# A selective scan that goes through two states in one instruction, over two adjacent PSUM banks

## The chip, the cores and the metric

The kernel runs on one core of a Trainium2 chip. The time is the device time of one execution in microseconds (us). A core has five engines with an instruction queue each, which run side by side and wait for one another through semaphores: TensorE (PE) multiplies matrices into PSUM, VectorE (DVE) and ScalarE (ACT) work on SBUF and PSUM, GpSimd (POOL) works on SBUF only, and SyncE (SP) here issues all DMAs. Each queue is worked off in order: an instruction that waits holds up everything behind it on its engine.

## What is computed

Eight images of 96 channels and 64x64 points go through a hybrid block: layer norm, projection, depthwise convolution, a selective scan in four directions, gating, two small convolutions with a channel gate, then a linear attention and a feed-forward layer in 8-bit floats. Most of the time goes into the scan, which for every direction k, channel d (192) and state n (16) runs over the 4096 points:

```python
def step(hst, inp):
    u_i, dt_i, b_i, c_i = inp
    dA = jnp.exp(dt_i[..., None] * A)
    hst = dA * hst + (dt_i * u_i)[..., None] * b_i[:, :, None, :]
    y = jnp.einsum('bkdn,bkn->bkd', hst, c_i)
    return (hst, y)
...
ys = ys.transpose(1, 2, 3, 0) + D[None, :, :, None] * u
```

with `dt_i` a softplus of a projection (the step sizes, `delta`), and `A = -exp(A_logs)`. The four directions are forward and backward over two orders of the points; their results are added.

## The kernel before

**Units.** The scan part works in 256 units in a row: 8 images x 4 directions x 8 chunks of T = 512 points. A chunk continues the states of the chunk before it in its direction, except the first of each direction (`u.start`, 32 units). Channels lie 64 to a tile, and the two halves of the 128 partitions hold two different states of them; so 192 channels x 16 states are 24 rows of [128, 512], worked off in 24 **slots**. Slot 4n + m is state m (of G = 4) of tile n (of 6, `TILES`).

**One state.** ACT makes the decays `da` = exp(delta x A) into a PSUM bank (`decays`, L1062), two slots ahead of their use, into one of three banks in turn. POOL makes the scan's inputs `hb` = b x du for the four states of a tile at once (`inputs`, L946, into one of six buffers). DVE scans (L1123): h = da x h + hb along the 512 points; a backward unit walks the row from its end. The product with C is made in one of two ways. A **banked** state is scanned into its PSUM bank and multiplied by c on DVE into `hb` (L1125); an unbanked one is scanned into `hb`, and POOL multiplies all unbanked states of a tile together (`outputs`, L952). `BANKED` says how many states of each tile are banked: tiles 0, 2 and 4 wholly, 1 and 3 not at all, tile 5 one or two, which makes 13 banked states in the first 8 units of all images but the first, and 14 in all others. The last column of each state is kept by ACT in `carry` (L1126 for one banked state, L1131 for the unbanked states of a tile), for the next chunk. PE sums `hb` over states and halves into the banks y01 and y2 (`sums`, L972), adds the skip term or the other directions' result (L981, fetched by `before`), and ACT copies them out (`gather`, L989 and L992).

**Step sizes.** `step_sizes` has six parts: PE's matmul into a bank of its own, `dt` (L911), three ACT activations (L919, L921, L923), one DVE operation that reads the bank again (L925), and one POOL product with u (L928). Form "a" serves a unit, form "b" the last 64 channels of two units. `spread` copies the results by DMA to both halves (L940).

**Order.** Nothing is scheduled automatically: each engine gets its instructions in the order of the program. `plan` puts every step of a unit at a slot by hand; in each slot the scan comes first, then the planned steps, then one step of each **side stream**: the front of the next image and the back end of the last one (convolutions, norms, attention, feed-forward) are generators that yield how many slots to pause. They use the banks f0 and f1. [...]da 3, dt 1, f0, f1, y01, y2.

**DMA.** SP issues fetches in the program's order, and requests made with `later` three slots after.

Of the kernel before, what the change touches and what calls it, by code (L numbers as in the profile page):

```python
# [22 lines left out]
T = 512  # L23
# [7 lines left out]
SPREAD = 5  # L31
HB = 6

BANKED = ((4, 0, 4, 0, 4, 1), (4, 0, 4, 0, 4, 2))

HOLD = 3
LAND = 11
# [6 lines left out]
def kernel(ctx: ExitStack, tc: tile.TileContext, a, out):  # L44
# [13 lines left out]
    dram = ctx.enter_context(tc.tile_pool(name="scratch", bufs=2, space=DRAM))  # L58
    psum = ctx.enter_context(tc.tile_pool(name="psum", bufs=1, space=PSUM))

    BANKS = {"da": 3, "dt": 1, "f0": 1, "f1": 1, "y01": 1, "y2": 1}

    def bank(tag, name):
        return psum.tile([P, T], F32, tag=tag, name=name, bufs=BANKS[tag])
# [9 lines left out]

    eps = const([P, 1], 1e-5, "eps")
    one = const([P, 1], 1.0, "one")
    ones_c = const([C, C], 1.0 / C, "ones_c")

    def centering(n, m, diagonal, name):
# [766 lines left out]
    for b in range(out.shape[0]):  # L846
        s = {"b": b, "done": set(), "live": b + 1 == out.shape[0]}
        images.append(s)
        for pair in (1, 0):
            for back in range(2):  # L850
                for i in range(NC):
                    u = Unit()
                    u.s, u.pair, u.back, u.k = s, pair, back, pair + 2 * back
                    u.c, u.start = (NC - 1 - i if back else i), i == 0
                    u.new, u.i = (pair, back, i) == (1, 0, 0), len(units)
                    u.bc, u.hb, u.delta, u.du = {}, {}, {}, {}
                    u.banked = BANKED[int(b == 0 or u.i % 32 >= NC)]
                    units.append(u)

# [41 lines left out]
    def step_sizes(us, i):  # L901

        u, which = us[0], "ab"[len(us) - 1]
        if i == 0:
            u.ps = bank("dt", "dt")
            if which == "a":
                todo = [(u.ps, slice(0, P), u)]
            else:
                todo = [(u.ps[64 * h : 64 * h + 64], slice(P, DI), w) for h, w in enumerate(us)]
            for ps, d, w in todo:  # L910
                nc.tensor.matmul(ps, dt_w[32 * w.k : 32 * w.k + R + 1, d], w.dts, start=True, stop=True)  # L911
            u.nat = sp.tile([P, T], F32, tag="nat" + which, name="nat", bufs=1)
            if which == "a":
                u.nata = u.nat
            else:
                for w in us:
                    w.natb = u.nat
        elif i == 1:
            nc.scalar.activation(u.nat, u.ps, AF.Abs)  # L919
        elif i == 2:  # L920
            nc.scalar.activation(u.nat, u.nat, AF.Exp, scale=-1.0)  # L921
        elif i == 3:
            nc.scalar.activation(u.nat, u.nat, AF.Ln, bias=one)  # L923
        elif i == 4:
            nc.vector.scalar_tensor_tensor(u.nat, u.ps, 0.0, u.nat, ALU.max, ALU.add)  # L925
        else:
            x = u.ua if which == "a" else u.ub
            nc.gpsimd.tensor_tensor(x, u.nat, x, ALU.mult)  # L928
# [19 lines left out]
    def outputs(u, n):  # L948

        lo = u.banked[n]  # L950
        hb = u.hb[n][:, lo:, :]
        nc.gpsimd.tensor_tensor(hb, hb, u.bc[1, TILES[n][0]][:, lo:, :], ALU.mult)  # L952

    def before(u):

        src = u.s["u"][1] if u.k == 1 else u.s["y"][u.pair]
        u.plain = []
        for i, rows in enumerate((slice(0, P), slice(P, src.shape[0]))):
            t = sp.tile([P, T], F32, tag=f"u{i}", name=f"u{i}", bufs=1)[: rows.stop - rows.start]
            u.plain.append(into(t, src[rows, bass.ts(u.c, T)]))  # L960

    def sums(u, ns, m):

# [7 lines left out]
        for ps, n, i in todo:  # L971
            nc.tensor.matmul(  # L972
                ps, halves, u.hb[n][:, i, :], start=TILES[n][0] == 0 and m == 0, stop=False, skip_group_check=True
            )
        if ns[-1] == 5 and m == 1:
            first = u.k == 1
            for ps, w, x in (
                (u.p[0], dd_a if first else ident, u.plain[0]),
                (u.p[1][low] if first else u.p[1], dd_b if first else ident, u.plain[1]),
            ):  # L980
                nc.tensor.matmul(ps, w, x, start=False, stop=True, skip_group_check=True)  # L981

    def gather(u, i):

# [12 lines left out]
    def plan(u, last, nxt, third):  # L997

        at = [[] for _ in range(24)]

        def put(slot, f, *args):
            at[slot].append((f, args))

        if last:
            put(0, outputs, last, 5)
            put(0, before, last)
            for m in range(2):
                put(m, sums, last, (3, 4), 2 + m)
            for m in range(2):
                put(5 + m, sums, last, (5,), m)  # L1010
            put(7, states, u, 1, 1)
            put(10, gather, last, 0)
            put(11, gather, last, 1)
        for n in range(6):
            to = (u, n + 2) if n < 4 else (nxt, n - 4)
            if to[0]:
                put(4 * n + 1, inputs, *to)
        if third and u.i % 2:
            put(16, step_sizes, (nxt, third), 5)
        put(8, outputs, u, 1)  # L1020
        put(16, outputs, u, 3)
        for m in range(4):
            put(13 + m, sums, u, (0, 1), m)
            if m < 2:
                put(18 + m, sums, u, (2,), m)
                put(22 + m, sums, u, (3, 4), m)
        if nxt:
            for i, slot in enumerate((0, 2, 4)):
                put(slot, step_sizes, (nxt,), i + 3)
            put(4, spread, nxt, 0, (0, 1))  # L1030
            put(6, spread, nxt, 1, (0, 1))
            put(10, states, nxt, 0, 0)
            put(15, states, nxt, 1, 0)
            put(20, states, nxt, 0, 1)
            if u.i % 2 == 0:
                put(15, spread, nxt, 0, (2,))
                put(16, spread, nxt, 1, (2,))
        if third:
            put(1, fetched_dt, third)
            put(9, fetched_u, third)  # L1040
            for i, slot in enumerate((20, 22, 23)):
                put(slot, step_sizes, (third,), i)
            if u.i % 2:
                for i, slot in enumerate((9, 11, 12, 13, 15)):
                    put(slot, step_sizes, (nxt, third), i)
                put(17, spread, nxt, 0, (2,))
                put(18, spread, nxt, 1, (2,))
            elif u.i + 3 < len(units):
                put(21, fetched_pair, third, units[u.i + 3])
        return at  # L1050

    def at_index(i):
        return units[i] if 0 <= i < len(units) else None

    def decays(q):

        if q >= 24 * len(units):
            return
        u, (n, m) = units[q // 24], divmod(q % 24, G)
        g, j = TILES[n]  # L1060
        da[q] = bank("da", "da")
        nc.scalar.activation(  # L1062
            da[q], u.delta[j], AF.Exp, scale=a_neg[:, u.k, j, g * G + m : g * G + m + 1]
        )

    da, kept, side, carry = {}, [], [], None
    for u in units[:2]:
        fetched_dt(u)
    fetched_u(units[0])
# [6 lines left out]
    for what in range(2):  # L1076
        spread(units[0], what, range(3))
    fetched_u(units[1])
    for i in range(3):
        step_sizes(units[1:2], i)  # L1080
    inputs(units[0], 0)
    inputs(units[0], 1)
    decays(0)
    decays(1)

    def advance(n):

# [4 lines left out]
    for u in units:  # L1092
        last, nxt, third = (at_index(u.i + d) for d in (-1, 1, 2))
        if u.new:
# [7 lines left out]
            else:  # L1102
                final = back_end(b, u.s)
                last_kit = back_kit(None, "f0", True, kit_f)
                side.append(Stream(final[0][0](last_kit, range(1, NC)[::-1])))
        if third and third.new:
            drained(*side[-1:])
            all_issued()
        if u.start:
            carry = sp.tile([P, 24], F32, tag="carry", name="carry")  # L1110
        todo = plan(u, last, nxt, third)
        for slot in range(24):
            n, m = divmod(slot, G)
            g, j = TILES[n]
            q, hb, first_at = 24 * u.i + slot, u.hb[n], 0 if u.back else T - 1
            col = carry[:, 8 * j + g * G + m : 8 * j + g * G + m + 1]
            while kept:
                kept.pop(0)()
            decays(q + 2)
            d = da.pop(q)  # L1120
            banked = m < u.banked[n]
            dd, x = (d[:, ::-1], hb[:, m, ::-1]) if u.back else (d, hb[:, m, :])
            nc.vector.tensor_tensor_scan(dd if banked else x, dd, x, 0.0 if u.start else col, ALU.mult, ALU.add)  # L1123
            if banked:
                nc.vector.tensor_tensor(hb[:, m, :], d, u.bc[1, g][:, m, :], ALU.mult)  # L1125
                kept.append(lambda col=col, d=d, at=first_at: nc.scalar.copy(col, d[:, at : at + 1]))  # L1126
            elif m == G - 1:
                lo = 8 * j + g * G
                kept.append(
                    lambda c=carry[:, lo + u.banked[n] : lo + G].unsqueeze(2), h=hb[:, u.banked[n] :, :], at=first_at:  # L1130
                    nc.scalar.copy(c, h[:, :, at : at + 1])  # L1131
                )
            for f, args in todo[slot]:
                f(*args)
            place[0] = slot
# [2 lines left out]
    for f in kept:  # L1138
        f()
    outputs(u, 5)  # L1140
    before(u)
    for m in range(2):
        sums(u, (3, 4), 2 + m)
    for m in range(2):
        sums(u, (5,), m)
    gather(u, 0)
    gather(u, 1)
    all_issued()
# [76 lines left out]
```

## Time and profile before

| | us |
|---|---|
| median of 3 runs (lowest to highest) | 11356.66 (11348.54 to 11358.43) |
| the profiled execution | 11372.37 |
| its span, first to last instruction | 11370.7 |
| the scan part in it | 347 to 11090 |
| one image of 32 units, in the middle | 1352 (2990 to 4342) |
| DMA, share of the 16 engines, scan part | 0.85 |
| PE clock granted, mean | 0.82 |

A profile line of a group names the source line, the engine, the operation, output <- inputs and their shapes and the count; after the first bar the total busy time in us and the mean duration in ns; after the second the idle time of the engine just before these instructions and what ended most of it. A line in order of time begins with the start and the duration in us; "x4" at its end are four in a row. A waiting line reads: who waited, at which line, <- for whom, then total us, number of times and the longest.

### The profile page before, as it was taken

The numbers are of one execution on the slowest core, as the hardware profiler recorded it, in microseconds if no ns is written. First come the engines' busy times: TensorE is split into PE (matmuls) and PEld (weight loads), VectorE is DVE, ScalarE is ACT, GpSimd is POOL, SyncE is SP. The second block draws the span as 40 slices with busy tenths as digits, with TensorE's granted clock in tenths as the row PEclk, the third lists the DMA queues.
The fourth block names the chain that finished last, engine by engine and source line by source line (L and its number), as shares of the span: only waits on it lengthen the run. The fifth ranks groups of instructions, "written<-read, shape, count | busy, mean of one in ns | idle before, by whom it ended". The sixth has DMA issues, their size and how long they took to land. (4 is left out here: it accounts for less than half of the span.)

```text
span 11370.7 us, 97041 instructions
## 1 busy us (share of the span) xinstructions
PE 8567.3 (75%) x23270; PEld 2328.5 (20%) x23270; DVE 10367.4 (91%) x10828; ACT 7508.4 (66%) x14939; POOL 10398.7 (91%) x2783
## 2 busy tenths in 40 slices
PE   6577657887778877888678876788768887676677
PEld 2111112222122211222112221222212221111122
DVE  0799999999999999999999999999999999999991
ACT  3566656767666676667766676666766667666674
POOL 0799999999999999999999999999999999999990
PEclk8678778888788877889778887888878888787787
DMA  2788878898888888888888888889888888888872
GB/s 71 171 197 197 201 189 210 209 225 196 203 210 212 219 198 202 210 215 215 195 207 210 216 214 194 210 205 228 202 200 211 212 220 195 198 198 195 201 188 78
DMA packets 1081039, 2253.24 MB, mean 198 GB/s; under 512 B 419609, under 2 KB 420314, under 8 KB 949395
## 3 DMA queue, kind: packets, MB, share of 16 engines
q1 hardware_dynamic: 1080467, 2247.05, 81.3%
q8 instruction: 184, 3.01, 0.1%
q14 instruction: 388, 3.18, 0.1%
HBM read 1507.14 MB, written 336.69 MB: 162 GB/s over the span
## 5 line engine op out<-in xcount | busy, mean ns | idle before, releaser
L946 POOL TENSOR_TENSOR hb<-b,du 128x2048 f32<-128x2048 f32 x1536 | 6939.0, 4535 | 21.3 <-DMA du<-ua 14.3
L1062 ACT ACTIVATE da<-delta,w_a_logs 128x512 f32<-128x512 f32 x6144 | 4216.7, 689 | 696.3 <-DVE hb L1123 575.8
L972 PE MATMUL p<-hb,halves 128*64 128x512 f32 x12288 | 3822.7, 731 | 800.1 <-POOL hb L952 382.1
L1123 DVE TENSOR_TENSOR_SCAN da<-da,carry,hb 128x512 f32<-128x512 f32 x3087 | 3949.0, 1279 | 58.0 <-ACT da L1062 54.3
L952 POOL TENSOR_TENSOR hb<-hb,c 128x2048 f32<-128x2048 f32 (+2 forms) x768 | 2984.9, 3887 | 304.7 <-ACT carry L1131 252.2
L1123 DVE TENSOR_TENSOR_SCAN hb<-da,carry,hb 128x512 f32<-128x512 f32 x2289 | 2781.0, 1264 | 57.7 <-ACT da L1062 56.7
L1125 DVE TENSOR_TENSOR hb<-da,c 128x512 f32<-128x512 f32 x3528 | 2440.5, 692 | 154.0 <-DVE da L1123 0.9
L1126 ACT COPY carry<-da 128x1 f32<-128x1 f32 x3528 | 554.9, 157 | 2351.6 <-DVE hb L1125 2341.1
L972 PEld LDWEIGHTS p<-hb,halves 128*64 128x64 f32 x12288 | 916.2, 161 | 3540.7 <-issue 2129.5
L434 PE MATMUL conv<-f0im,taps 97*128 97x512 f32 (+1 forms) x2088 | 903.5, 664 | 95.9 <-ACT f0pre L490 54.3
L928 POOL TENSOR_TENSOR ua<-nat,ua 128x512 f32<-128x512 f32 x256 | 327.3, 1279 | 257.5 <-DMA b<-xd 257.5
L1123 DVE TENSOR_TENSOR_SCAN da<-da,hb 128x512 f32<-128x512 f32 x441 | 537.7, 1219 | 26.0 <-POOL hb L946 24.6
L925 DVE SCALAR_TENSOR_TENSOR nat<-dt,nat 128x512 f32<-128x512 f32 x384 | 259.5, 676 | 238.9 <-ACT nat L923 238.9
L911 PE MATMUL dt<-dts,dt_w 7*64 7x512 f32 (+1 forms) x1024 | 450.0, 657 | 16.9 <-DVE nat L925 12.4
L981 PE MATMUL p<-u,ident 128*128 128x512 f32 x768 | 438.3, 699 | 3.6 <-DMA u<-y 3.6
L376 PE MATMUL ctr<-f1b,cen_c 96*96 96x512 f32 x460 | 271.9, 697 | 193.4 <-DVE f1b L769 158.8
L434 PEld LDWEIGHTS conv<-f0im,taps 97*128 97x128 f32 (+1 forms) x2088 | 254.6, 174 | 681.6 <-issue 523.5
L1123 DVE TENSOR_TENSOR_SCAN hb<-da,hb 128x512 f32<-128x512 f32 x327 | 377.9, 1204 | 4.9 <-ACT da L1062 4.9
L382 PE MATMUL var<-f1b,ones_c 96*96 96x512 f32 x346 | 207.4, 684 | 153.6 <-ACT f1b L379 145.3
L792 POOL TENSOR_TENSOR f1b<-f1b,f1o 96x512 f32<-96x512 f32 x58 | 67.7, 1167 | 252.0 <-ACT f1o L790 251.9
L1131 ACT COPY carry<-hb 128x4 f32<-128x4 f32 (+2 forms) x768 | 146.8, 191 | 197.4 <-DVE hb L1123 184.8
L655 PE MATMUL cab<-f1m,cab_w 96*96 96x512 f32 x348 | 206.0, 719 | 90.9 <-ACT f1b L664 41.4
(416 smaller groups left out, 7710.5 us busy)
## 6 DMA issues: line engine op xcount, KB each, us to landing
b<-xd SPq DMA_DIRECT2D x1024, 512.0 KB
c<-xd SPq DMA_DIRECT2D x1024, 512.0 KB
delta<-nat SPq DMA_DIRECT2D x1536, 128.0 KB
du<-ua SPq DMA_DIRECT2D x1024, 128.0 KB
y<-yt SPq DMA_DIRECT2D x512, 256.0 KB
u<-y SPq DMA_DIRECT2D x384, 256.0 KB
ua<-u SPq DMA_DIRECT2D x256, 256.0 KB
du<-ub SPq DMA_DIRECT2D x512, 128.0 KB
```

Of the source, the lines that this page charges most:

```text
L376: nc.tensor.matmul(ps, cen_c, src, start=i == 0, stop=i == len(srcs) - 1)
L434: nc.tensor.matmul(ps, taps[:, t, lo : lo + n], im[:, r0 + dy : r0 + dy + 8, dx : dx + HW], start=t == 0, stop=t == 8,)
L911: nc.tensor.matmul(ps, dt_w[32 * w.k : 32 * w.k + R + 1, d], w.dts, start=True, stop=True)
L928: nc.gpsimd.tensor_tensor(x, u.nat, x, ALU.mult)
L946: nc.gpsimd.tensor_tensor(hb, u.bc[0, g], u.du[j].unsqueeze(1).to_broadcast([P, G, T]), ALU.mult)
L952: nc.gpsimd.tensor_tensor(hb, hb, u.bc[1, TILES[n][0]][:, lo:, :], ALU.mult)
L972: nc.tensor.matmul(ps, halves, u.hb[n][:, i, :], start=TILES[n][0] == 0 and m == 0, stop=False, skip_group_check=True)
L981: nc.tensor.matmul(ps, w, x, start=False, stop=True, skip_group_check=True)
L1062: nc.scalar.activation(da[q], u.delta[j], AF.Exp, scale=a_neg[:, u.k, j, g * G + m : g * G + m + 1])
L1123: nc.vector.tensor_tensor_scan(dd if banked else x, dd, x, 0.0 if u.start else col, ALU.mult, ALU.add)
L1125: nc.vector.tensor_tensor(hb[:, m, :], d, u.bc[1, g][:, m, :], ALU.mult)
L1126: kept.append(lambda col=col, d=d, at=first_at: nc.scalar.copy(col, d[:, at : at + 1]))
```

## The change

Two neighbouring states (slots q and q + 1, q even) become one piece of work. The decays of a pair lie in one PSUM tile of two adjacent banks, and there are two such tiles, four banks; the bank `dt` is given up, and the step sizes' matmul uses y01 (form "a") or y2 (form "b") in the slots between the copy-out of the last unit's sums and the first sums of this one. One scan instruction runs over both states, 1024 elements. So that the second state in walking order doesn't continue the first, ACT sets the decay at its first point to zero, after it has put that point's share of the kept state into the input: hb += decay x carry (one-element Identity with pointers for scale and bias, then a one-element copy of a zero). In a starting unit there is no kept state and no Identity. A banked pair's product is one instruction over 1024 elements, and its two last columns are kept by one copy. `decays(q + 2)` still stands ahead of the scan of slot q, and so makes the next pair. `BANKED` goes to 14 banked states in the first 8 units of all images but the first and 16 elsewhere, where tile 5 is banked wholly and its `outputs` falls away. In `plan` the copies-out go from slots 10 and 11 to 5 and 8, the step sizes of form "a" into the slots 7 to 20 of one unit, and the fetches that feed them, the spreads and the fetch of the plain results (split in two) to other slots.

```diff
-BANKED = ((4, 0, 4, 0, 4, 1), (4, 0, 4, 0, 4, 2))
+BANKED = ((4, 0, 4, 0, 4, 2), (4, 0, 4, 0, 4, 4))
...
-    BANKS = {"da": 3, "dt": 1, "f0": 1, "f1": 1, "y01": 1, "y2": 1}
+    BANKS = {"f0": 1, "f1": 1, "y01": 1, "y2": 1}
...
-            u.ps = bank("dt", "dt")
+            u.ps = bank({"a": "y01", "b": "y2"}[which], "dt")
...
     def outputs(u, n):
         lo = u.banked[n]
+        if lo == G:
+            return
...
-        da[q] = bank("da", "da")
-        nc.scalar.activation(
-            da[q], u.delta[j], AF.Exp, scale=a_neg[:, u.k, j, g * G + m : g * G + m + 1]
-        )
+        d = da[q] = psum.tile([P, 2, T], F32, tag="da", name="da", bufs=2)
+        for i in range(2):
+            scale = a_neg[:, u.k, j, g * G + m + i : g * G + m + i + 1]
+            nc.scalar.activation(d[:, i, :], u.delta[j], AF.Exp, scale=scale)
+        i, at = (0, T - 1) if u.back else (1, 0)
+        edge, at = d[:, i, at : at + 1], slice(at, at + 1)
+        if not u.start:
+            x, col = u.hb[n][:, m + i, at], column(j, g, m + i)
+            nc.scalar.activation(x, edge, AF.Identity, bias=x, scale=carry[0][:, col : col + 1])
+        nc.scalar.copy(edge, zero)
...
+    def scanned_pair(u, slot):
+        n, m = divmod(slot, G)
+        g, j = TILES[n]
+        q, hb = 24 * u.i + slot, u.hb[n]
+        end = slice(0, 1) if u.back else slice(T - 1, T)
+        while kept:
+            kept.pop(0)()
+        decays(q + 2)
+        d, x = da.pop(q), hb[:, m : m + 2, :]
+        banked = m < u.banked[n]
+        dd, xx = (t.rearrange("p m l -> p (m l)") for t in (d, x))
+        if u.back:
+            dd, xx = dd[:, ::-1], xx[:, ::-1]
+        col = column(j, g, m + u.back)
+        init = 0.0 if u.start else carry[0][:, col : col + 1]
+        nc.vector.tensor_tensor_scan(dd if banked else xx, dd, xx, init, ALU.mult, ALU.add)
+        if banked:
+            nc.vector.tensor_tensor(x, d, u.bc[1, g][:, m : m + 2, :], ALU.mult)
+            states_of, lo, hi = d, m, m + 2
+        elif m == G - 2:
+            states_of, lo, hi = hb[:, u.banked[n] :, :], u.banked[n], G
+        else:
+            return
+        to = carry[0][:, column(j, g, lo) : column(j, g, hi)].unsqueeze(2)
+        kept.append(lambda: nc.scalar.copy(to, states_of[:, :, end]))
...
 # in plan: slots of the steps that move
-            put(0, before, last)
+            put(3, added, last, 0)
+            put(5, gather, last, 0)
...
+            put(6, added, last, 1)
+            put(8, gather, last, 1)
...
-            put(10, gather, last, 0)
-            put(11, gather, last, 1)
+            put(2, spread, nxt, 0, (0, 1))
+            put(3, spread, nxt, 1, (0, 1))
...
+            put(6, fetched_u, third)
+            for i, slot in enumerate((7, 9, 10, 11, 13, 20)):
+                put(slot, step_sizes, (third,), i)
+            if u.i % 2:
+                for i, slot in enumerate((9, 11, 12, 13, 15, 16)):
+                    put(slot, step_sizes, (nxt, third), i)
...
-        for m in range(4):
-            put(13 + m, sums, u, (0, 1), m)
+        for m, slot in enumerate((14, 15, 16, 16)):
+            put(slot, sums, u, (0, 1), m)
...
+        put(19, before, u, 0)
+        put(21, before, u, 1)
...
-            for i, slot in enumerate((0, 2, 4)):
-                put(slot, step_sizes, (nxt,), i + 3)
-            put(4, spread, nxt, 0, (0, 1))
-            put(6, spread, nxt, 1, (0, 1))
...
-            put(1, fetched_dt, third)
-            put(9, fetched_u, third)
-            for i, slot in enumerate((20, 22, 23)):
-                put(slot, step_sizes, (third,), i)
...
+            put(14, fetched_dt, fourth)
...
-            for f, args in todo[slot]:
+            if slot % 2 == 0:
+                scanned_pair(u, slot)
+            for f, args in todo[slot]:
```

`added` is the identity matmul of the plain results, which stood at the end of `sums` before.

More of the change, by code (lines that the diff above doesn't have):

```diff
@@ L76 @@
     one = const([P, 1], 1.0, "one")
+    zero = const([P, 1], 0.0, "zero")
     ones_c = const([C, C], 1.0 / C, "ones_c")
@@ L855 @@
                     u.new, u.i = (pair, back, i) == (1, 0, 0), len(units)
-                    u.bc, u.hb, u.delta, u.du = {}, {}, {}, {}
+                    u.bc, u.hb, u.delta, u.du, u.plain = {}, {}, {}, {}, {}
                     u.banked = BANKED[int(b == 0 or u.i % 32 >= NC)]
@@ L950, in outputs, with before, added @@
         lo = u.banked[n]
+        if lo == G:
+            return
         hb = u.hb[n][:, lo:, :]
         nc.gpsimd.tensor_tensor(hb, hb, u.bc[1, TILES[n][0]][:, lo:, :], ALU.mult)
-    def before(u):
+    def before(u, i):
         src = u.s["u"][1] if u.k == 1 else u.s["y"][u.pair]
[L957 to L960, printed above, removed]
+        rows = (slice(0, P), slice(P, src.shape[0]))[i]
+        t = sp.tile([P, T], F32, tag=f"u{i}", name=f"u{i}", bufs=1)[: rows.stop - rows.start]
+        u.plain[i] = into(t, src[rows, bass.ts(u.c, T)])
+    def added(u, i):
+        ps, first = u.p[i], u.k == 1
+        w = ((dd_a, dd_b)[i]) if first else ident
+        nc.tensor.matmul(
+            ps[0:64] if first and i else ps, w, u.plain[i], start=False, stop=True, skip_group_check=True
+        )
     def sums(u, ns, m):
@@ L974, in sums @@
             )
[L975 to L981, printed above, removed]
     def gather(u, i):
@@ L1005, in plan @@
             put(0, outputs, last, 5)
-            put(0, before, last)
             for m in range(2):
                 put(m, sums, last, (3, 4), 2 + m)
+            put(3, added, last, 0)
+            put(5, gather, last, 0)
             for m in range(2):
                 put(5 + m, sums, last, (5,), m)
+            put(6, added, last, 1)
+            put(8, gather, last, 1)
             put(7, states, u, 1, 1)
-            put(10, gather, last, 0)
-            put(11, gather, last, 1)
+        if nxt:
+            put(2, spread, nxt, 0, (0, 1))
+            put(3, spread, nxt, 1, (0, 1))
+        if third:
+            put(6, fetched_u, third)
[4 more added lines that the diff above has]
+                    put(slot, step_sizes, (nxt, third), i)
         for n in range(6):
@@ L1017, in plan @@
                 put(4 * n + 1, inputs, *to)
-        if third and u.i % 2:
-            put(16, step_sizes, (nxt, third), 5)
         put(8, outputs, u, 1)
         put(16, outputs, u, 3)
-        for m in range(4):
-            put(13 + m, sums, u, (0, 1), m)
+        for m, slot in enumerate((14, 15, 16, 16)):
+            put(slot, sums, u, (0, 1), m)
             if m < 2:
@@ L1037, in plan @@
                 put(16, spread, nxt, 1, (2,))
-        if third:
-            put(1, fetched_dt, third)
-            put(9, fetched_u, third)
-            for i, slot in enumerate((20, 22, 23)):
-                put(slot, step_sizes, (third,), i)
-            if u.i % 2:
-                for i, slot in enumerate((9, 11, 12, 13, 15)):
-                    put(slot, step_sizes, (nxt, third), i)
+            else:
                 put(17, spread, nxt, 0, (2,))
                 put(18, spread, nxt, 1, (2,))
-            elif u.i + 3 < len(units):
-                put(21, fetched_pair, third, units[u.i + 3])
+        fourth = at_index(u.i + 3)
+        if fourth:
+            put(14, fetched_dt, fourth)
+            if u.i % 2 == 0:
+                put(21, fetched_pair, third, fourth)
         return at
@@ L1053, in at_index, with column @@
         return units[i] if 0 <= i < len(units) else None
+    def column(j, g, m):
+        return 8 * j + g * G + m
     def decays(q):
@@ L1060, in decays @@
         g, j = TILES[n]
-        da[q] = bank("da", "da")
-        nc.scalar.activation(
-            da[q], u.delta[j], AF.Exp, scale=a_neg[:, u.k, j, g * G + m : g * G + m + 1]
-        )
-    da, kept, side, carry = {}, [], [], None
+        d = da[q] = psum.tile([P, 2, T], F32, tag="da", name="da", bufs=2)
[8 more added lines that the diff above has]
+        nc.scalar.copy(edge, zero)
+    da, kept, side, carry = {}, [], [], [None]
     for u in units[:2]:
@@ L1078 @@
     fetched_u(units[1])
-    for i in range(3):
-        step_sizes(units[1:2], i)
     inputs(units[0], 0)
@@ L1083 @@
     decays(0)
-    decays(1)
+    for i in range(6):
+        step_sizes(units[1:2], i)
+    fetched_dt(units[2])
+    def scanned_pair(u, slot):
[19 more added lines that the diff above has]
+            states_of, lo, hi = hb[:, u.banked[n] :, :], u.banked[n], G
+        else:
+            return
+        to = carry[0][:, column(j, g, lo) : column(j, g, hi)].unsqueeze(2)
+        kept.append(lambda: nc.scalar.copy(to, states_of[:, :, end]))
     def advance(n):
@@ L1105 @@
                 side.append(Stream(final[0][0](last_kit, range(1, NC)[::-1])))
-        if third and third.new:
+        if u.i + 3 < len(units) and units[u.i + 3].new:
             drained(*side[-1:])
@@ L1109 @@
         if u.start:
-            carry = sp.tile([P, 24], F32, tag="carry", name="carry")
+            carry[0] = sp.tile([P, 24], F32, tag="carry", name="carry")
         todo = plan(u, last, nxt, third)
         for slot in range(24):
[L1113 to L1132, printed above, removed]
+            if slot % 2 == 0:
+                scanned_pair(u, slot)
             for f, args in todo[slot]:
@@ L1140 @@
     outputs(u, 5)
-    before(u)
     for m in range(2):
@@ L1145 @@
         sums(u, (5,), m)
+    for i in range(2):
+        added(u, i)
     gather(u, 0)
```

## The prediction

> **What bounds the kernel now.** I read the page's first part, then busy times by stretch of one image, then groups by shape, then the order of time on VectorE (DVE), then the waits.
>
> ```profile
> PE 8567.3 (75%) x23270; PEld 2328.5 (20%) x23270; DVE 10367.4 (91%) x10828; ACT 7508.4 (66%) x14939; POOL 10398.7 (91%) x2783
> ```
>
> Two engines stand at 91%. The scan part runs from 347 to 11090 us, 10,743 us for 256 units, and the rest (627 us) is prelude and end, which the change leaves alone. One image (32 units) in quarters of 8 units:
>
> ```profile
> core 0: us, PE busy (x) PEld busy (x) DVE busy (x) ACT busy (x) POOL busy (x), PEclk, DMA share, GB/s
> 2990.00:3340.00 350.00, 272.52 (x676) 70.32 (x672) 329.77 (x344) 228.01 (x467) 332.21 (x86) 0.84 0.85 209
> 3340.00:3674.00 334.00, 281.21 (x838) 72.19 (x838) 318.73 (x328) 232.07 (x443) 321.76 (x85) 0.88 0.88 214
> 3674.00:4016.00 342.00, 280.97 (x806) 83.46 (x806) 324.98 (x346) 234.42 (x477) 320.66 (x86) 0.86 0.87 214
> 4016.00:4342.00 326.00, 228.44 (x592) 57.57 (x592) 320.64 (x331) 240.83 (x485) 325.72 (x92) 0.75 0.82 196
> ```
>
> After the stretch and its length the columns are busy time and, in brackets, instructions. DVE and POOL are both at 93.7% or more in every quarter; in the last one POOL is full (325.7 of 326) and DVE all but. ACT stands near 70%. Prices, from the groups by shape:
>
> ```profile
> L946 POOL TENSOR_TENSOR hb<-b,du 128x2048 f32<-128x2048 f32 x1536 | 6939.0, 4535 | 21.3 <-DMA du<-ua 14.3
> L1062 ACT ACTIVATE da<-delta,w_a_logs 128x512 f32<-128x512 f32 x6144 | 4216.7, 689 | 696.3 <-DVE hb L1123 575.8
> L1126 ACT COPY carry<-da 128x1 f32<-128x1 f32 x3528 | 554.9, 157 | 2351.6 <-DVE hb L1125 2341.1
> ```
>
> Durations overlap or leave gaps, so I take steps from start to start:
>
> ```profile
> 3411.29 1.28 DVE L1123 TENSOR_TENSOR_SCAN da<-da,carry,hb 128x512 f32<-128x512 f32 x1
> 3412.60 0.69 DVE L1125 TENSOR_TENSOR hb<-da,c 128x512 f32<-128x512 f32 x1
> 3413.21 1.28 DVE L1123 TENSOR_TENSOR_SCAN da<-da,carry,hb 128x512 f32<-128x512 f32 x1
> ...
> 3432.74 4.80 DVE L1123 TENSOR_TENSOR_SCAN hb<-da,carry,hb 128x512 f32<-128x512 f32 x4
> 3437.46 1.26 DVE L1123 TENSOR_TENSOR_SCAN da<-da,carry,hb 128x512 f32<-128x512 f32 x1
> ```
>
> A banked state (scan into PSUM, product with C on DVE) takes 1.31 + 0.61 = 1.92 us of DVE; an unbanked one (product on POOL) 4.72/4 = 1.18. A unit with 14 banked states takes 14 x 1.92 + 10 x 1.18 = 38.7 us, plus 1.5 step-size operations of 0.6, plus 1 to 2 us of the other streams: 40.5 to 41 against the 40.8 to 43.7 of the quarters. POOL, in the same order of time: eight operations at 4.48 (two inputs in a row took 8.97), one over two states at 2.33, 1.5 step-size products at 1.23: 40.0. What DVE and ACT wait for:
>
> ```profile
> DVE hb L1123 <- ACT da L1062: 61.6, 90, 1.4
> DVE da L1123 <- ACT da L1062: 54.3, 22, 6.0
> ...
> ACT carry L1126 <- DVE hb L1125: 2341.1, 2311, 4.1
> ```
>
> The columns are total us, times and longest. Today ACT waits for DVE; DVE waits for decays only 116 us.
>
> [...]
>
> **The change, part by part.**
>
> *Pairs on DVE.* A second state in the same instruction costs only its length. Banked pair: (1.31 + 1.07) + (0.61 + 0.53) = 3.52 instead of 3.84. Unbanked pair: 1.18 + 1.07 = 2.25 instead of 2.36. BANKED moves work from POOL too: 200 units go from 14 to 16 banked states, 56 units (3528 = 200 x 14 + 56 x 13) from 13 to 14. DVE per unit: 38.7 to 8 x 3.52 + 4 x 2.25 = 37.2 in the 200; 37.9 to 7 x 3.52 + 5 x 2.25 = 35.9 in the 56. Sum: 200 x 1.52 + 56 x 2.05 = 419 us less. All of it is on the path. No run shows a 1024 scan over two banks; if the fixed part were per element, 0 would be saved in pairing, and the moved products would cost (456 x 0.74) 340 us more.
>
> *POOL.* The 2.33 operation goes from 200 units and a 3.4 becomes 2.33 in 56: 528 us less, 37.7 and 40.0 per unit. It falls below DVE in the 200. In the 56, DVE has 35.9 + 0.9 + about 3 of the back end, so both stay level.
>
> *ACT, the added work.* Per pair one 1-element Identity with two pointers ([...]the 157 ns of the copy bounds it below; I take 0.35; none in the 32 starting units, so 2688) and one 1-element copy of zero (0.19, as the carry copies from SBUF), 3072. Carry copies fall from 3528 to 1992. Sum 941 + 584 - 292: about +1.2 ms on 7.3 ms, 80% of the scan part. Busy time alone costs nothing.
>
> *ACT, the added wait.* This is the disputed term. Before, three single banks: a decay had two slots to be made in. After, two double banks: those of pair p+1 start when pair p-1 is finished (product included), and are due when p ends. Chain: 0.62 + 0.70 (two decays, the second drained) + 0.35 + 0.19 + two handshakes of 0.04 = 1.94 us, 2.13 with the carry copy before it. DVE gives it 3.52 in a banked pair, 2.25 in an unbanked one. Behind it in ACT's queue stand all evacuations, norms and step-size activations (0.77 us per pair on average: 7284 - 4217 - 701 over 3072), and DVE stands behind it. A norm (two activations, 1.2 us) or Silu with two table loads (1.28 each, 1.48) does not fit beside an unbanked pair. Laying ACT's list beside DVE's in the changed order: ACT's is longer in 996 of 3060 pairs, by 858 us together; what even the slack of the following pair can't take up is 189. These are the ends. Arrears of neighbouring pairs add up and ACT also waits for PE (195 us today), so I take twice the lower, 380; the 116 of today are in it, so +265.
>
> *Identity waits for POOL's hb one pair earlier.* Behind it stand the zero copy and DVE. In the stretch after 3398 the tightest tile is ready 4.1 us ahead of its scan (3419.7 against 3423.9); the Identity comes 2.2 us ahead at most. Cost 0; if POOL is late by more, each microsecond is on the path (25 us today, most at the start).
>
> *Step sizes in y01/y2.* The matmul at slot 7 waits for the evacuation at slot 5, p's first matmuls at slot 14 for DVE's operation at slot 13. Behind the latter on PE are the sums that free hb for POOL at slot 17. POOL waits 7 us for them today. I take 0; its end is 2 us in each of 256 units. The dt fetch, u fetch and the plain-y fetches are only moved earlier or a slot pair away on SP, whose waits for nat (1952 us) go; nothing is due there. DMA stands at 0.85 share and would go to 0.86.
>
> *Side streams.* They advance in both slots of a pair, so half of their DVE operations directly follow ACT work of the same pair. DVE waits some 145 us for those now; I add a third, 45.
>
> Sum: -419 + 265 + 45 = -109. The profiled execution took 11372.4 us (span 11370.7), so 11263; it lies 16 above the median of 11356.7, so 11245.
>
> **Rivals.**
> 1. Forecast: DVE's saving arrives, two thirds are eaten by ACT. 11245 (11130 to 11330). Chance 0.45.
> 2. ACT keeps ahead, as its 66% suggest: -419 and hardly any new stall, 10960. Against it: 2.25 against 1.94. Chance 0.17.
> 3. ACT's chain becomes the bound in the unbanked tiles: the whole 858 is paid, less today's 116, plus 45: 11357 - 419 + 787 = 11725 at worst; 463 of the 858 lie in banked pairs, and with half of that absorbed it is 11494. I take 11500. It decides from 419 + 116 = 535 us of DVE waits for ACT, 2.1 per unit. For it: DVE waits up to 6 us for a decay already today. Chance 0.28, slower.
> 4. Pairing saves no DVE time, or PE's later sums bind POOL: the gain of 419 is void, about 11357. [...] Chance 0.10.
>
> **How the numbers follow.** A run can tell 0.2%, 23 us, from no change. Faster: 0.42 of rival 1, all of 2, 0.01 of 4: 0.60. Same: 0.03 + 0.02 + 0.05 = 0.10. Slower: 0.26 + 0.04 = 0.30. The range goes from the full saving (10950) to a little above rival 3, where a third of the banked pairs' 463 is absorbed (11571, cut to 11560).
>
> **What would show it.** Right: scans of 1024 at 2.35 us (products 1.22), 3072 of them; POOL at least 1 us per unit freer in the later quarters; DVE waiting 300 to 450 us for ACT, most in slots 4 to 7 and 12 to 15. Wrong: those waits under 200 or over 535 us; scans over 2.5 us; POOL or PE waits of more than 100 us more than now.

## The result, and the profile after

| | us |
|---|---|
| before, median of 4 runs (lowest to highest) | 11357.55 (11348.54 to 11363.57) |
| after, median of 4 runs (lowest to highest) | 11542.52 (11536.19 to 11544.22) |
| ratio, 95% interval | 1.0163 (1.0145 to 1.018) |
| profiled execution after, its span | 11542.72, 11541.0 |

The changed kernel is 1.6% slower; the forecast was 1.0% faster. The time lies within the range, but on the other side of no change.

The page's first line of the kernel after: PE, DVE and POOL have less to do, and ACT more.

```profile
PE 8504.1 (74%) x23270; PEld 2330.4 (20%) x23270; DVE 10069.0 (87%) x6221; ACT 8816.3 (76%) x18963; POOL 9883.1 (86%) x2583
```

DVE fell from 10367.4 to 10069.0 us and POOL from 10398.7 to 9883.1, yet the span grew. Over the scan part alone, now 347 to 11260 us:

```profile
core 0: us, PE busy (x) PEld busy (x) DVE busy (x) ACT busy (x) POOL busy (x), PEclk, DMA share, GB/s
347.00:11260.00 10913.00, 8086.50 (x22186) 2191.55 (x22186) 9987.35 (x6074) 8573.68 (x18594) 9841.86 (x2545) 0.82 0.82 202
```

The same view of before, over 347 to 11090:

```profile
347.00:11090.00 10743.00, 8143.79 (x22236) 2185.41 (x22238) 10311.60 (x10696) 7283.64 (x14612) 10376.00 (x2748) 0.82 0.85 205
```

So DVE is busy for 324 us less and idle for 495 us more (926 against 431): 171 us longer. The short gaps ahead of the products shrank by 54 us as well (from 154 to 100, the idle times at the end of these two lines, before and after):

```profile
L1125 DVE TENSOR_TENSOR hb<-da,c 128x512 f32<-128x512 f32 x3528 | 2440.5, 692 | 154.0 <-DVE da L1123 0.9
```

```profile
L1122 DVE TENSOR_TENSOR hb<-da,c 128x1024 f32<-128x1024 f32 x1992 | 2440.0, 1225 | 100.1 <-issue 0.4
```

So the real new waiting is 495 + 54 = 549 us. One image in quarters of 8 units, chosen at the same work as those of before:

```profile
3036.00:3388.00 352.00, 269.06 (x662) 71.81 (x662) 314.96 (x197) 266.93 (x593) 318.66 (x84) 0.82 0.82 206
3388.00:3734.00 346.00, 276.51 (x838) 72.02 (x838) 313.39 (x187) 275.15 (x571) 305.78 (x78) 0.90 0.85 207
3734.00:4079.00 345.00, 281.97 (x812) 84.35 (x814) 314.37 (x202) 274.02 (x599) 300.88 (x78) 0.86 0.83 210
4079.00:4415.00 336.00, 220.76 (x598) 56.60 (x594) 312.57 (x187) 283.93 (x607) 311.49 (x85) 0.78 0.78 193
```

No engine is full any more: DVE stands at 89 to 93% of a quarter where it had 94 to 98%, and POOL at 87 to 93%. The 27 us that this image loses lie in all its quarters, though unevenly (2, 12, 3 and 10 us), and are not one event. The groups of the pair's instructions, by shape:

```profile
L1120 DVE TENSOR_TENSOR_SCAN da<-da,carry,hb 128x1024 f32<-128x1024 f32 x1743 | 4096.1, 2350 | 272.7 <-ACT da L1082 118.0
...
L1120 DVE TENSOR_TENSOR_SCAN hb<-da,carry,hb 128x1024 f32<-128x1024 f32 x945 | 2206.7, 2342 | 319.6 <-ACT da L1082 302.8
...
L1129 ACT COPY carry<-da 128x2 f32<-128x2 f32 x1992 | 314.4, 158 | 1329.6 <-DVE hb L1122 1321.3
L1081 ACT ACTIVATE hb<-da,hb,carry 128x1 f32<-128x1 f32 x2688 | 944.9, 352 | 177.1 <-ACT da L1076 5.2
...
L1082 ACT COPY da<-zero 128x1 f32<-128x1 f32 x3072 | 500.1, 163 | 96.8
```

The two operations on ACT cost 352 and 163 ns, about as priced. What they set off stands at the end of the scans' lines: their idle time is ended by L1082, the copy of zero. ACT's own wait for DVE at the carry copy fell from 2341 to 1321 us, so ACT has 1,020 us less of slack there. DVE in order of time, a banked pair, then two unbanked ones:

```profile
1089.11 2.35 DVE L1120 TENSOR_TENSOR_SCAN da<-da,carry,hb 128x1024 f32<-128x1024 f32 x1
1091.50 1.22 DVE L1122 TENSOR_TENSOR hb<-da,c 128x1024 f32<-128x1024 f32 x1
1092.64 4.68 DVE L1120 TENSOR_TENSOR_SCAN hb<-da,carry,hb 128x1024 f32<-128x1024 f32 x2
1097.75 2.36 DVE L1120 TENSOR_TENSOR_SCAN da<-da,carry,hb 128x1024 f32<-128x1024 f32 x1 [0.43 <-ACT da L1082]
```

From start to start the banked pair takes 3.53 us (predicted 3.52). In brackets is a wait of 0.43 us for ACT. The largest waits of DVE in the scan part of the kernel after:

```profile
DVE hb L1120 <- ACT da L1082: 318.1, 239, 4.8
DVE da L1120 <- ACT da L1082: 121.7, 151, 2.2
DVE f1b L572 <- ACT f1b L571: 88.8, 55, 3.9
DVE da L1120 <- issue: 62.1, 96, 2.6
DVE da L1120 <- ACT carry L1129: 53.4, 50, 4.5
```

With 15.5 us more of the carry kind, the scans wait 509 us for ACT's decays and carries, and 62 us more where the profile names nobody. Before it was 116. One of the longer stalls, ACT's queue first:

```profile
1262.10 0.16 ACT L1082 COPY da<-zero 128x1 f32<-128x1 f32 x1
1262.20 0.58 ACT L994 COPY yt<-p 128x512 f32<-128x512 f32 x1
1262.79 1.28 ACT L398 ACT_TABLE_LOAD   x1
1264.09 1.48 ACT L443 ACTIVATE f0pre<-f0pre 128x1536 f32<-128x1536 f32 x1
1265.59 1.28 ACT L398 ACT_TABLE_LOAD   x1
1266.88 0.60 ACT L920 ACTIVATE nat<-dt 128x512 f32<-128x512 f32 x1
1267.38 0.15 ACT L1129 COPY carry<-da 128x2 f32<-128x2 f32 x1
1267.56 1.42 ACT L1076 ACTIVATE da<-delta,w_a_logs 128x512 f32<-128x512 f32 x2
1269.07 0.35 ACT L1081 ACTIVATE hb<-da,hb,carry 128x1 f32<-128x1 f32 x1
1269.46 0.16 ACT L1082 COPY da<-zero 128x1 f32<-128x1 f32 x1
```

```profile
1265.83 1.22 DVE L1122 TENSOR_TENSOR hb<-da,c 128x1024 f32<-128x1024 f32 x1
1269.72 2.35 DVE L1120 TENSOR_TENSOR_SCAN hb<-da,carry,hb 128x1024 f32<-128x1024 f32 x1 [2.67 <-ACT da L1082]
```

Between one pair's chain and the next stand a copy-out, a Silu with its two table loads and a step-size activation, 5.2 us in one piece. Only then come the carry copy and the four instructions of the next pair, 2.2 us, and DVE, which was done with its product by then, stands for 2.67 us. With two buffers of a pair each there is nothing made ahead that it could scan meanwhile.

### The profile page after: what moved, and what is told of

It is laid out like the page before. It is cut to its first block, busy times and chain, and to the rows that moved or that the text cites. A ratio compares the mean times of both kernels' runs of the same rounds, so it can differ in the third digit from the quotient of the medians.

```text
span 11541.0 us, 97703 instructions
## 1 busy us (share of the span) xinstructions
PE 8504.1 (74%) x23270; PEld 2330.4 (20%) x23270; DVE 10069.0 (87%) x6221; ACT 8816.3 (76%) x18963; POOL 9883.1 (86%) x2583
## 5 line engine op out<-in xcount | busy, mean ns | idle before, releaser
L947 POOL TENSOR_TENSOR hb<-b,du 128x2048 f32<-128x2048 f32 x1536 | 6922.5, 4526 | 76.0 <-PE p L981 38.0
L1120 DVE TENSOR_TENSOR_SCAN da<-da,carry,hb 128x1024 f32<-128x1024 f32 x1743 | 4096.1, 2350 | 272.7 <-ACT da L1082 118.0
L955 POOL TENSOR_TENSOR hb<-hb,c 128x2048 f32<-128x2048 f32 (+1 forms) x568 | 2449.7, 4313 | 833.7 <-issue 539.0
L1122 DVE TENSOR_TENSOR hb<-da,c 128x1024 f32<-128x1024 f32 x1992 | 2440.0, 1225 | 100.1 <-issue 0.4
L1120 DVE TENSOR_TENSOR_SCAN hb<-da,carry,hb 128x1024 f32<-128x1024 f32 x945 | 2206.7, 2342 | 319.6 <-ACT da L1082 302.8
L1129 ACT COPY carry<-da 128x2 f32<-128x2 f32 x1992 | 314.4, 158 | 1329.6 <-DVE hb L1122 1321.3
L1081 ACT ACTIVATE hb<-da,hb,carry 128x1 f32<-128x1 f32 x2688 | 944.9, 352 | 177.1 <-ACT da L1076 5.2
L912 PE MATMUL dt<-dts,dt_w 7*128 7x512 f32 (+1 forms) x1024 | 526.6, 777 | 461.6 <-ACT yt L994 242.0
L1120 DVE TENSOR_TENSOR_SCAN da<-da,hb 128x1024 f32<-128x1024 f32 x249 | 569.4, 2287 | 7.7 <-ACT da L1082 3.7
L1082 ACT COPY da<-zero 128x1 f32<-128x1 f32 x3072 | 500.1, 163 | 96.8
L1120 DVE TENSOR_TENSOR_SCAN hb<-da,hb 128x1024 f32<-128x1024 f32 x135 | 304.7, 2277 | 15.3 <-ACT da L1082 15.3
```

The source lines that it names most:

```text
L947: nc.gpsimd.tensor_tensor(hb, u.bc[0, g], u.du[j].unsqueeze(1).to_broadcast([P, G, T]), ALU.mult)
L1081: nc.scalar.activation(x, edge, AF.Identity, bias=x, scale=carry[0][:, col : col + 1])
L1082: nc.scalar.copy(edge, zero)
L1120: nc.vector.tensor_tensor_scan(dd if banked else xx, dd, xx, init, ALU.mult, ALU.add)
L1122: nc.vector.tensor_tensor(x, d, u.bc[1, g][:, m : m + 2, :], ALU.mult)
```

## The experiments

The cause was open between two readings: the chain of one pair is too long for the time that DVE leaves it (the edge operations must be *waited for*), or ACT's in-order queue is so full that any work in it delays the decays (the edge operations only *take room*). Beside these, the pairs themselves, the new plan or `BANKED` might be the loss. All figures in us are a ratio's distance from 1 times 11,350, so that kernels of different series can be set side by side; a ratio's interval is some 8 to 20 us to each side. The change itself is +185 (165 to 204).

**No edge operations.** The Identity and the copy of zero are left out, so the second state of a pair goes on from the first. The kernel no longer computes the reference and serves for its time alone.

```diff
-        i, at = (0, T - 1) if u.back else (1, 0)
-        edge, at = d[:, i, at : at + 1], slice(at, at + 1)
-        if not u.start:
-            x, col = u.hb[n][:, m + i, at], column(j, g, m + i)
-            nc.scalar.activation(x, edge, AF.Identity, bias=x, scale=carry[0][:, col : col + 1])
-        nc.scalar.copy(edge, zero)
```

> Leaves out the Identity and the zero copy, so the second state of a pair goes on from the first. Before took 11357 us, after 11542. Theory A (the two edge operations make ACT's chain for a pair 2.1 us against 2.25 us of an unbanked pair on DVE, and the arrears stop DVE): the chain falls to 1.5 us, DVE's waits for ACT's decays from some 510 us to 150, time 11180. Theory B (the look-ahead is what is missing: two double tiles instead of three single ones, whatever the chain): waits stay above 350, time 11390. Theory C (six or three step-size activations now stand together in slots 9 to 13): waits fall by half, the rest stays in slots 8 to 16, time 11300.

11114.01 us, ratio 0.9793 (0.9778 to 0.9807): -235. The two tiny operations cost 420 us, more than the whole loss. DVE's waits in the scan part of this kernel:

```profile
DVE hb L1114 <- ACT da L1076: 172.8, 177, 3.9
DVE f1b L572 <- ACT f1b L571: 74.8, 43, 3.9
DVE da L1114 <- ACT da L1076: 32.5, 43, 1.6
```

205 us of waiting for decays remain even so; "Four single banks" below takes this up.

**Two scans of 512 in the pair's frame.** As the one above, but each state is scanned by itself.

```diff
+        for i in range(2):
+            dd, xx = (t[:, i, ::-1] if u.back else t[:, i, :] for t in (d, x))
+            col = column(j, g, m + i)
+            init = 0.0 if u.start else carry[0][:, col : col + 1]
+            nc.vector.tensor_tensor_scan(dd if banked else xx, dd, xx, init, ALU.mult, ALU.add)
```

> Keeps the paired decays, products and banks, but scans each state on its own with its own start value, so that no edge operation is needed; computes the whole reference. DVE pays 0.11 to 0.14 us more per pair, 3072 pairs, some 360 us; ACT is free of 1445 us of edge work. Theory A: 11180 as without edges plus 360 less what the waits leave over, 11480. Theory B: 11600. Theory C: 11550.

11630.05, ratio 1.0246 (1.0231 to 1.0261): +279, 514 us above the kernel without edges, whose scans are paired. That is 514 / 3072 = 0.167 us per pair. In order of time the pair's two scans reach its product after 2.64 us instead of 2.39:

```profile
1087.42 2.61 DVE L1113 TENSOR_TENSOR_SCAN da<-da,carry,hb 128x512 f32<-128x512 f32 x2
1090.06 1.23 DVE L1115 TENSOR_TENSOR hb<-da,c 128x1024 f32<-128x1024 f32 x1
```

By the prediction's steps, 2 x 1.31 against 2.38 us in the 1992 banked pairs and 2.36 against 2.25 in the 1080 others, some 600 us were to be saved, so pairing saves most of what the prediction said, and the first half of rival 4 falls. The time lies nearest to what was expected if too little look-ahead were the cause (11600), but for another reason: DVE is busy for 528 us more than without edges (10553.3 against 10025.7), where 360 were expected, while its scans wait for decays 162 us, less than the 205 there.

**The plan alone.** The old scans and `BANKED` with three single banks, but the new plan, with the step sizes in the sums' banks.

```diff
-    BANKS = {"f0": 1, "f1": 1, "y01": 1, "y2": 1}
+    BANKS = {"da": 3, "f0": 1, "f1": 1, "y01": 1, "y2": 1}
...
-            if slot % 2 == 0:
-                scanned_pair(u, slot)
+            n, m = divmod(slot, G)
```

> The kernel before in its scans, decays (three single banks) and BANKED, with the new places of the step sizes, fetches and copies-out alone. Theories A and B: 11357 give or take 25. Theory C: the crowd in slots 9 to 13 costs by itself, partly covered by the two slots of look-ahead: 11420 or more.

11246.77, ratio 0.9912 (0.9896 to 0.9929): -100. The step that I priced at nothing is a gain. PE does wait anew, 154 us for the copies-out at the step sizes' matmul (433 in the kernel after), but DVE does not wait for more because of it. DVE waits for decays 58 us:

```profile
DVE hb L1136 <- ACT da L1074: 35.6, 45, 2.6
...
DVE da L1136 <- ACT da L1074: 22.0, 23, 2.8
```

**Earlier copies-out alone**, in the kernel before, the one part of the new plan that could be moved by itself:

```diff
-            put(10, gather, last, 0)
-            put(11, gather, last, 1)
+            put(7, gather, last, 0)
+            put(8, gather, last, 1)
```

> The kernel before with the two copies-out of the last unit's sums at slots 7 and 8 instead of 10 and 11, nothing else. The new plan alone (with single scans) took 102 us off. In the kernel before 92 us of DVE's scan waits lie in slots 11 to 15, where ACT had the two copies, 0.58 or 1.09 us each, beside form b's activations; with the new plan 27 us are left there. If the place of the copies is the cause: 11260 to 11310. If it is another part of the plan: 11357 give or take 20.

11323.25, ratio 0.9979 (0.9972 to 0.9986): -24, between the two expectations. That is a quarter of the plan's 100; where the rest comes from stays open.

**14 banked states in all units but the first 8 of an image.** The changed kernel with the last tile's `BANKED` back at 2.

> The changed kernel with 14 banked states in all units (before: 13 or 14; changed: 14 or 16). In 200 units one pair goes from banked, 3.53 us of DVE, to unbanked, 2.25: 256 us less DVE; POOL gets 2.33 us more in each, 40.0 per unit. Theory A and C: DVE has less time beside ACT's chain in slots 20 to 23, waits for ACT rise by some 50 us, and POOL at 40 us per unit plus its waits stands level with DVE: 11500 to 11600. If DVE's own work were the bound: 11300.

11512.19, ratio 1.014 (1.0124 to 1.0155): +159, with an interval that overlaps the change's own. The new `BANKED` is not where the loss comes from.

**The edge operations put aside**, to tell room from waiting. In the first try both wrote to spare columns, but the Identity still read `hb` and the carry:

```diff
-            nc.scalar.activation(x, edge, AF.Identity, bias=x, scale=carry[0][:, col : col + 1])
-        nc.scalar.copy(edge, zero)
+            nc.scalar.activation(aside[0], one, AF.Identity, bias=x, scale=carry[0][:, col : col + 1])
+        nc.scalar.copy(aside[1], zero)
```

> The changed kernel with the same two one-element ACT operations per pair in the same place of ACT's queue, but writing to spare columns in SBUF and reading none of the pair's decays, so that no scan waits for them; leaves out the break between the two states of a pair. ACT is as busy as in the changed kernel (11542), the chain to the scan is as short as without them (11114). If the length of the chain is what costs: 11114 to 11250. If ACT's occupancy is (every operation delays all later ones): 11450 or more.

11415.62, ratio 1.0052 (1.0037 to 1.0067): +59. It tells nothing: an unbanked scan writes the `hb` that the Identity reads, so DVE still waited 287 us for the operation put aside. The second try reads constants only (`bias=one, scale=eps`), so that nobody waits for either:

> As the run with the edge operations aside (11416), but the Identity reads constants only; there it still read the pair's hb, which the scan writes over, so that unbanked scans waited for it (287 us of waits for the spare columns). Leaves out the break between the two states of a pair. Now no DVE instruction waits for the two operations, and ACT's queue is as full as in the changed kernel. If the wait for the chain is the larger part of the 428 us that the edge operations cost: below 11300. If the fullness of ACT's queue is: 11330 or more.

11302.94, ratio 0.9963 (0.9948 to 0.9978): -42. ACT has the same 18,963 instructions as after, but no engine has to wait for the two put aside. First the page's line of busy times, then the waits:

```profile
PE 8447.9 (75%) x23270; PEld 2306.5 (20%) x23270; DVE 10042.0 (89%) x6223; ACT 8413.6 (74%) x18963; POOL 9882.2 (87%) x2583
```

```profile
DVE hb L1118 <- ACT da L1077: 233.0, 242, 3.2
DVE da L1118 <- ACT da L1077: 104.2, 121, 4.1
```

It is 193 us above the kernel without them (-42 against -235), and 227 below the change. It lies between the two expectations, and both readings hold: 193 us are *room* (337 us of waiting for decays instead of 205, the rest at the side streams' operations), and 227 us come from waiting for the chain. The halves are not sharply cut: ACT is busy for 402 us less here than after (8414 against 8816), for in order of time the operations put aside overlap with what stands ahead of them. The Identity begins 0.06 us before the two decays end, where in the kernel after it begins 0.09 us behind them, and from the start of the two decays to the end of the copy it is 1.80 us where the kernel after takes 2.06 (in the queue shown above):

```profile
1087.40 1.42 ACT L1077 ACTIVATE da<-delta,w_a_logs 128x512 f32<-128x512 f32 x2
1088.76 0.37 ACT L1079 ACTIVATE aside<-one,eps 128x1 f32<-128x1 f32 x1
1089.03 0.17 ACT L1080 COPY aside<-zero 128x1 f32<-128x1 f32 x1
```

So 193 is a lower end of the room, and some of the 227 is room too.

**Less crowding on ACT.** The step sizes of form "b" go from slots 9, 11, 12, 13, 15 and 16 to 9, 12, 14, 16, 17 and 18, and their spreads to 19 and 20.

> The changed kernel with the step sizes of form b moved to slots 9, 12, 14, 16, 17, 18 (before: 9, 11, 12, 13, 15, 16) and their spreads two slots on. Some 480 of 607 us of the changed kernel's scan waits lie in slots 8 to 16. If the crowd of step-size activations there causes them: 150 to 250 us less, 11340. If edge operations alone do: 11520.

11417.66, ratio 1.0055 (1.004 to 1.007): +62, so 123 us of the loss go by moving five small steps and two spreads of every second unit, less than the 150 to 250 expected. By my count over the order of time, the scans' waits in the kernel after lie mostly in the pairs at slots 8 to 16 (481 of 607 us), where the new plan has up to six step-size activations in slots 9 to 13; here those at slot 14 fall from 204 to 81.

**Four single banks.** The plan alone, with the four banks of the two pairs as four single ones.

> Single scans with the new places (11247 with three single banks), and the bank that the step sizes have given up as a fourth single bank for decays; made two slots ahead as before. If the look-ahead in banks limits: some 50 us less, 11200. If not (DVE's waits for decays are 58 us there, and the order of ACT's queue is unchanged): 11247 give or take 25.

11190.8, ratio 0.9855 (0.9841 to 0.987): -165. The scans wait 38 us for decays:

```profile
DVE hb L1136 <- ACT da L1074: 19.2, 16, 2.4
DVE da L1136 <- ACT da L1074: 18.5, 15, 2.7
```

The same four banks as two pairs, without edge operations, had 205. Of the 378 us that pairing and `BANKED` take off DVE, only 135 arrive (-100 to -235). I put this down to the coarser grain: pairs give back a bank only when both states are done. That is argued and not shown, for no run separates it from two other differences. DVE comes back for decays sooner when it has less to do. And by my count over the order of time, ACT begins the second decay of a pair 0.72 us after the first, where two decays in a row into single banks begin 0.62 us apart; over 3072 pairs that is, as an estimate, 0.3 ms of ACT's time.

**The edges once per unit.** If room and chain are the loss, the break between the states must leave ACT's chain. For every scan row the decay at the unit's first point depends on `delta` there. So ACT makes all 8 edge decays of a channel group in one small exp, then sets that first point of `delta` to 1e6, so that every decay made from it is zero. POOL multiplies the edge decays by the carry and adds them to the first column of `hb`; every scan starts from 0.

```diff
+        if not u.start:
+            e, at = u.edge[j], first(u)
+            if g == 0:
+                nc.gpsimd.tensor_tensor(e, e, carry[0][:, 8 * j : 8 * j + 8], ALU.mult)
+            x = hb[:, :, at]
+            nc.gpsimd.tensor_tensor(x, x, e[:, g * G : g * G + G].unsqueeze(2), ALU.add)
...
+    def edges(u, j):
+        d = u.delta[j][:, first(u)]
+        if not u.start:
+            u.edge[j] = sp.tile([P, 2 * G], F32, tag="edge", name="edge", bufs=6)
+            nc.scalar.activation(u.edge[j], a_neg[:, u.k, j, :], AF.Exp, scale=d)
+        nc.scalar.copy(d, huge)
```

> Pairs without edge operations per pair; computes the whole reference. Per unit and 64 channels ACT makes the first point's 8 decays at once and then sets delta's first column to a huge number, so that all decays there are zero; POOL multiplies them with the kept states and adds the product to the first column of hb, nine small operations per unit; all scans start from zero. ACT's chain is that of the run without edges (11114), plus 1.4 us of ACT per unit aside, some 1 to 2 us of POOL per unit, and 0.06 us less DVE per scan without the start value (some 160 us). If the chain is the cause and POOL's slack holds: 10980 to 11130. If small POOL operations cost over 0.3 us each: 11300.

11113.15, ratio 0.9785 (0.9769 to 0.9801): -244, the same as without any edge. It computes the whole reference and beats both kernels. Its line of busy times, then two of its groups:

```profile
PE 8475.2 (76%) x23270; PEld 2311.3 (21%) x23270; DVE 9911.3 (89%) x6221; ACT 7712.9 (69%) x14643; POOL 10234.4 (92%) x4599
```

```profile
L954 POOL TENSOR_TENSOR hb<-hb,edge 128x4 f32<-128x4 f32 x1344 | 269.5, 200 | 105.3
...
L952 POOL TENSOR_TENSOR edge<-edge,carry 128x8 f32<-128x8 f32 x672 | 139.1, 207 | 10.3 <-ACT carry L1142 10.2
```

ACT is relieved of 1.1 ms (8816 to 7713), and POOL, which the change had freed of 515 us, takes up 409 of them. The scans now wait for POOL's edges 67 us and for decays 253.

**Two variants of it**: one with less crowding, and one with 16 banked states in all units and the crowding of the first.

> Edges made once per unit (11113) with the step sizes of form b less crowded (slots 9, 12, 14, 16, 17, 18), which took 125 us off the changed kernel. Of the waits with unit edges, 247 us lie in slots 12 to 16. If the crowd costs by itself, without the edge operations too: 11010 to 11070. If it only cost where ACT was full of edge operations: 11113 give or take 25.

11108.54, ratio 0.9789 (0.9772 to 0.9805): -239.

> Edges once per unit (11113) with 16 banked states in all units, the first 8 of an image too, where POOL now has 40.0 + 1.8 us per unit. POOL gets 2.3 us less and DVE 1.27 us more in 56 units. If POOL sets the pace in these: some 50 us less. If DVE with the back end's operations does: 70 us more.

11117.85, ratio 0.9803 (0.9788 to 0.9818): -224. Neither can be told from the first, and the second gave neither the 50 us less nor the 70 more that were expected. The crowding that cost 123 us while ACT was at 76% costs nothing that these runs can tell at 69%.

## Why the prediction was wrong

| term | predicted | measured |
|---|---|---|
| pairs and `BANKED` on DVE | -419 | -378 (324 of busy time, 54 of gaps) |
| POOL, busy time | -528 | -534 |
| ACT, busy time | about +1200 | +1290 |
| scans waiting for ACT, total | 380 | 509, and 62 unnamed |
| side streams and other waits | +45 | about +60, and some 35 in small ones |
| moved steps of the plan | 0 | -100 when made alone |

**The pairs**: right in kind and nearly in size. Scans of 1024 took 2.35 us, products 1.22, 3072 pairs; a second state adds 1.08 us to a scan, from start to start (2.39 - 1.31), and 0.53 us to a product (1225 against 692 ns). No run had shown the 1.07 and 0.53 of the prediction when it was made; these groups do. Since no engine but ACT has more to do, the loss is in the waits.

**The step that failed is "ACT, the added wait".** It laid the chain of 2.13 us (2.24 in the queue shown above, where the two handshakes put at 0.04 us are 0.09 and 0.04, and 0.10 us more pass before the scan begins) beside DVE's 3.52 and 2.25, found 189 and 858 as ends, and took twice the lower, 380. Measured are 509, or 571 with the 62 where nobody is named, on either side of the 535 from which rival 3 was said to decide: 393 to 455 us of new waiting where the sum has 265. Rival 3's 11500 is nearest to the measured time, but in part by luck: it has only the wait for the chain, which accounts for 227 of the 420 us that the edge operations cost, and it does not know of the 100 us that the plan gains. I see two reasons why 380 was too low. First, the sentence ahead of it, "Busy time alone costs nothing", is false at this fill: the operations put aside, for whose results nobody waits, cost 193 us. With the work of one pair as its whole look-ahead, ACT at 74 to 76% passes bursts of side work on to DVE, as in the stall of 2.67 us above. Second, part of the slack that was to absorb arrears was not there: pairs without edge operations already wait 205 us for decays, where three single banks wait 58 and four 38. I had read the free time of ACT (2341 us waiting at the carry copy) as a reserve; that copy belongs to banked states, and most of the waits are in unbanked pairs (318 of the 440 us that L1082 ends).

**Where the waits lie**: predicted in slots 4 to 7 and 12 to 15. Slots 12 to 15 hold (295 of 607 us by my count), 4 to 7 hardly count (39), and 8 to 11 and 16 (186) I had not named: there, I take it, the step sizes' activations meet the chain.

**The Identity waiting for POOL, priced at 0**: right. In the kernel after, the Identity waits 3.4 us in all for POOL's inputs. **Step sizes in the sums' banks**, priced at 0: harmless (POOL waits 38 us for the later sums, where it waited 7), and the plan as a whole gained 100; earlier copies-out alone gave 24 in the kernel before. **POOL or PE waits** as a sign against me were badly chosen: POOL waits 539 us at `outputs` with no releaser named, which it did not before, but it has become an engine with slack; it was busy for 534 us less.

**Slips in the sums.** The median of 11,357 less 109 is 11,248 and not 11,245, and the carry copies that fall away were priced at 0.19 us where the line shown has 0.157, which is 50 us of ACT's busy time. Neither changes the argument.

Put together in the order of the experiments: plan -100, pairs -135, room +193, chain +227, which is +185.

## What to carry to other kernels

An engine that runs in order (in the stall above, 5.2 us of other work ahead of a pair's chain on ACT left DVE standing for 2.67 us) and feeds the bound engine with a short look-ahead is to be priced by how its work lies, not by its busy share: two operations of 0.35 and 0.16 us per pair cost 420 us here, 193 of it even when nobody waited for their results. Wider buffers on the same banks may take back part of what the longer instruction saves: four banks held as two pairs had 205 us of waits for decays here, as four single ones 38, though no run shows that the coarser look-ahead is the cause. Where a break between rows is needed, look for the place where it can be made once for many rows, on an engine that the change has just freed.

## What the runs showed of the hardware

- A scan of 1024 fp32 elements took 2.34 us where it wrote to SBUF and 2.35 where it wrote across two PSUM banks (the kernel after); two of 512 in a row into PSUM took 2.61. One scan instruction fewer per pair saved 0.167 us per pair in the run's time.
- POOL did an operation on 4 elements per partition in 200 ns and on 8 in 207 (edges once per unit), against 4526 for 2048 (the kernel after): the 2016 small ones took 409 us in all.
- An ACT table load took 1.28 us. In the stall above the load begins 0.01 us after the copy ends, and the Silu 0.02 us after the load.
